# Regrouping the filler steps of a four-layer transformer stack: values' sums off VectorE, a norm moved beside the channel mix, more keys beside norms, keys summed in PSUM banks

## The chip, the core and the metric

The kernel runs on one core of one Trainium2 chip, all in float32. The metric is the device time of one execution in microseconds (us). Five engines work side by side, each through its own queue in order: TensorE (PE, with its weight loads shown as PEld), VectorE (DVE), ScalarE (ACT), GpSimd (POOL) and SyncE (SP, which issues all DMAs here). A float32 matmul shows in the profile as two records.

## What is computed

The tokens `x` are 8 sequences of 112 tokens with 512 channels, and the context is 8 x 375 x 512. Four layers follow one another:

```python
x = layer0(x, ctx)        # one-head cross attention, x + alpha * delta
x = layer1(x, state=ctx)  # RWKV block: time mix, then channel mix
x = layer2(x, state=ctx)  # the same, other weights
x = layer3(x, ctx)        # two cross attentions and an MLP
# an RWKV block
xa = ln(x); sx = shift(xa) - xa
xw, xk, xv, xr, xg = (xa + sx * (maa_f + tanh((xa + sx*maa_x) @ w1) @ w2[f]) for f in "wkvrg")
w = exp(-exp(decay + tanh(xw @ d1) @ d2)); r, k, v = xr @ Wr.T, xk @ Wk.T, xv @ Wv.T; g = silu(xg @ Wg.T)
s = k[:, None] * v[None, :] + w[:, None] * s      # per token, 32 heads of 16 x 16
x = x + group_norm(r @ (u * k v + s)) * g @ Wo.T
xc = ln(x); x = x + sigmoid(xr2 @ fWr.T) * (relu(xk2 @ fWk.T)**2 @ fWv.T)
# layer 3, twice, then the MLP: 16 heads of 128; one extra key and value (bias_k, bias_v)
h = ln(x); x = x + softmax((h @ wq + bq) @ keys.T / sqrt(128)) @ values @ wo + bo
x = x + gelu(ln(x) @ w_fc1 + b1) @ w_fc2 + b2
```

## The kernel before

Channels lie on the 128 partitions, in four blocks; tokens lie along the rows. The 896 tokens are worked on in two halves of 448 (`NH`), each of four sequences.

**Values and keys of layer 3.** They depend on the context alone. So `values()` (L788) is a generator that makes them early, and its steps are drawn one at a time as filler (`fill(n)`, L119) wherever layers 1 and 2 leave TensorE without work. Products of 2 x 2 blocks are made with seven block products in place of eight (the sums of weights and of context blocks that this needs are made beforehand). A unit of seven steps is k1, k6, k7 (one bank that keeps growing, copied by ACT at each step), k2, k8, and k5 and k9 (`last_two`, L895), which run between the first steps of the unit after. Two banks take turns. The sum for k2 is an ACT copy and a POOL addition (L966, L967); those for k5 and k9 are DVE additions that read the bank (L898, L902). Results go to DRAM (`store`). When the weights change, `relay` (L820) replaces them piece by piece: each of its stages (POOL sums L829 to L845, loads L807) is issued in the program right after the step that it names (`after`, L919).

**The scan.** `time_mix` (L538) has 64 steps per layer. Each multiplies a broadcast row of v by k (DVE, L675, `kv`, from a PSUM copy `vp` made by ACT, L576 and L577), runs the recurrence along tokens (DVE, L679, `st`), multiplies by r (POOL, L683, `rs`) and sums on TensorE (L656). About two filler steps are drawn in each. Here the order on each engine is the order of the program; elsewhere a scheduler sets each engine's order at build time from what is ready.

**Turned weights.** Wg and Wv of layers 1 and 2 have their columns put into another order in blocks of 128 x 128: a copy by ACT (L407) and a reordering copy back by POOL (L408), 32 of each per layer.

**Mixing.** `mixes(h, fills)` (L416) makes the norm and the five mixed inputs of one half. For the second half the filler is the first half's own projections, and `fills` says how many steps are drawn at each place.

**Channel mix and layer 3.** `channel_mix` (L708) ends with eight groups of output matmuls fv. Then `layer3` starts, with new tile pools. `attention` (L1084) normalizes x in two halves (`layer_norm_half`, L163) with filler from `first_keys`: the 14 steps of the keys of one pair of batches, made by `seven` (L1004): two banks in turn, two ACT copies and five DVE additions for each half of the rows. Eight batches follow for each of four groups of heads; in each, 4 heads go through scores (L1201), softmax (L206), transposes (L1204) and the product with the values (L1214). The key steps of later pairs run in between.

Of the kernel before, what the change touches and what calls it, by code (L numbers as in the profile page):

```python
# [108 lines left out]
def tile_kernel(ctx: ExitStack, tc: tile.TileContext, d: dict, out: bass.AP):  # L109
# [22 lines left out]
    ident = const.tile([P, P], F32, name="ident")  # L132
    make_identity(nc, ident)
# [18 lines left out]
    def project(ps, w, rhs, evacuate, name, hs=(0, 1)):  # L152

        for h in hs:
            for o in range(NC):
                p = mm(ps, f"ps_{name}_{o}_{h}")[:, :NH]
                for k in range(NC):
                    nc.tensor.matmul(
                        p, w[:, k, o * P : (o + 1) * P], rhs(k, h), start=k == 0, stop=k == NC - 1
                    )  # L160
                evacuate(o, h, p)

    def layer_norm_half(ps, work, y, h, scale, offset, name, room=None, bank=None, fills=(2, 2, 4), small_tag="rstd"):  # L163

        def small(tag, what):
            if room is not None:
# [23 lines left out]
        nc.vector.tensor_mul(y, y, rstd.unsqueeze(1).to_broadcast([P, NC, NH]))  # L192
        for c in range(NC):
            nc.scalar.activation(
                y[:, c, :], y[:, c, :], AF.Identity, bias=column(offset, c), scale=column(scale, c)
# [20 lines left out]
    def layer0():  # L216
# [3 lines left out]
        with (  # L220
# [4 lines left out]
        ):  # L225
            w_q, w_k = weight("L0_xattn_w_q"), weight("L0_xattn_w_k")
# [144 lines left out]
    def time_mix_inputs(n, pre, names, ones_t, first, k, v, r, g, decay, rows):  # L371
# [7 lines left out]
        with (  # L379
# [22 lines left out]
            for f in "gv":  # L402
                for o in range(NC):
                    for c in range(NC):
                        w = ws[f][:, c, o * P : (o + 1) * P]
                        t = work.tile([P, NH], F32, tag="e", name=f"turn{f}{n}_{o}_{c}")[:, :P]
                        nc.scalar.copy(t, w)  # L407
                        nc.gpsimd.tensor_copy(w.rearrange("p (q h r) -> p q h r", q=4, h=HB), turned(t))  # L408
# [49 lines left out]
            def projections(h, xw, xg):  # L458
# [4 lines left out]
                td = one.tile([P, NH], F32, tag="td", name=f"td{n}_{h}")  # L463
# [68 lines left out]
            following = projections(1, *mixes(1, (2, 1, 2, 1, 1, 0, 0, 0)))  # L532
# [175 lines left out]
    def channel_mix(n, pre, names, first):  # L708
        with (
# [49 lines left out]
            project(ps, f_v, lambda c, h: halves(kk[:, c, :], h), add, f"fv{n}")  # L759

    def rwkv_layers():
        with tc.tile_pool(name="rc", bufs=1) as one:
# [5 lines left out]
            with tc.tile_pool(name="rs", bufs=1) as setup:  # L768
# [8 lines left out]
                nc.vector.tensor_sub(less_mean_h, ident, mean_h)  # L777
# [10 lines left out]
    def values():  # L788
# [31 lines left out]
        def relay(at, old, new):  # L820
# [5 lines left out]
            for y, o, k in ((a11, 0, 0), (a21, 1, 0), (a22, 1, 1)):  # L826
                raw(y, at, o, k)
            yield "k1"
# [9 lines left out]
            new.update(k1=a11, k6=old["k6"], k7=old["k1"], k2=old["k7"], k8=old["k8"], k5=old["k9"], k9=old["k2"])  # L838
# [55 lines left out]

        def last_two(u, f, u2, u3, s, at):  # L895
            p = bank(u, f, f"k5_{u}")
            product(p, block(at), s["k5"])
            nc.vector.tensor_add(u3, p, u3)  # L898
# [3 lines left out]
            nc.vector.tensor_add(u2, p, u2)  # L902
# [14 lines left out]
        before, steps, following = iter(()), iter(()), None  # L917

        def after(what):  # L919
            nonlocal following  # L920
            if what == following:
# [9 lines left out]
        for u, (at, unit) in enumerate(units):  # L931
# [13 lines left out]
            elif unit == UNITS - 1 and at != 1:  # L945
                following = ready
            if unit % 3 == 0:
# [16 lines left out]

            y = shaped(pool.tile([P, C], F32, tag="k2", name=f"k2_{u}"), f)
            nc.scalar.copy(y, p)  # L966
            nc.gpsimd.tensor_add(p1, y, p1)  # L967
# [14 lines left out]
    def weight_sums(pool, tag, w, u):  # L982


        if tag == "wv":
            y = pool.tile([P, NC, C], F32, tag=tag, name=f"ws{u}")
# [74 lines left out]

    def quarters(y):
# [21 lines left out]
    def attention(i, h_in, work, kv, ps, ps2, keep, mlp_norm):  # L1084
# [9 lines left out]
        def key_pieces(gr, b, w, kts):  # L1094
# [3 lines left out]
            if ("wk", i, gr, b) in shared:  # L1098
                for j in range(2):
                    kts.append(kv.tile([P, HG, T], F32, tag="kt", name=f"k{u}_{j}", bufs=3))  # L1100
# [4 lines left out]
            cx = kv.tile([P, NC, S], F32, tag="cx", name=f"cx{u}", bufs=2)  # L1105
# [8 lines left out]
            kt = [kv.tile([P, HG, T], F32, tag="kt", name=f"k{u}_{j}", bufs=3) for j in range(2)]  # L1114
            kts += kt

            def put(j, o, p, y):
                dst = kt[j][:, o, :S]
                if y is None:
                    nc.scalar.copy(dst, p)  # L1120
# [298 lines left out]
```

## Time and profile before

| | us |
|---|---|
| median of 3 runs | 3005.23 |
| lowest, highest | 2998.66, 3009.64 |
| the profiled execution, its time | 3006.6 |
| the profiled execution, its span | 3004.8 |
| PE busy in it | 2874.8 |
| DVE busy | 1713.4 |
| ACT busy | 862.4 |
| POOL busy | 732.9 |

The rough order in the span: layer 0 up to 159 us, layer 1's mixing up to 364, its scan to 632, its output and channel mix to 801, the same for layer 2 with its scan from 1003 to 1282 and its end at 1470, the two attentions of layer 3 from there, with the second norm at 2127, and the MLP from about 2810. A row of the instructions in order of time gives start, length, engine, line, operation, output and inputs, the count, and in brackets how long the engine was idle before it and what released it. A row of waits gives the total, the number and the longest. A stage's row gives busy times and, after them, the clock that TensorE was granted as a share of full speed.

### The profile page before, as it was taken

How to read it: one execution, taken by the hardware profiler on the slowest of the kernel's cores; microseconds unless marked ns; L12 is line 12 of the kernel's file. 1: busy time of each engine (PE TensorE's matmuls, PEld its weight loads, DVE VectorE, ACT ScalarE, POOL GpSimd, SP SyncE). 2: the span in 40 equal slices, each digit the busy share in tenths (PEclk: the TensorE clock that was granted, in tenths of full speed). 3: DMA queues.
4: the chain of work that ended last, by engine and by line, in shares of the span. 5: the costliest groups of instructions: out<-in, count | busy, mean ns of one | idle time of the engine just before them, and what ended most of it. 6: DMA issues, size and time to landing. Idle time of an engine off the chain costs nothing.

```text
span 3004.8 us, 29759 instructions
## 1 busy us (share of the span) xinstructions
PE 2874.8 (96%) x10130; PEld 1571.3 (52%) x10130; DVE 1713.4 (57%) x2588; ACT 862.4 (29%) x1750; POOL 732.9 (24%) x636
## 2 busy tenths in 40 slices
PE   8989999998999998999899999999899999999999
PEld 4734443343444433346456666656465666656544
DVE  1464198956343588844366555646755565646455
ACT  2123354423243344422132122212221221212311
POOL 3142057534221366632200101020001001010030
PEclk9989999999999999999999999999999999999999
DMA  7421398843311788744225252434243433432110
GB/s 252 148 88 45 122 291 264 250 129 118 95 62 55 223 240 264 229 137 132 85 87 169 90 165 96 138 105 145 70 128 106 138 117 121 139 102 90 45 57 25
DMA packets 199319, 402.91 MB, mean 134 GB/s; under 512 B 33288, under 2 KB 119592, under 8 KB 192384
## 3 DMA queue, kind: packets, MB, share of 16 engines
q1 hardware_dynamic: 199168, 401.01, 42.9%
q8 instruction: 81, 1.33, 0.2%
q14 instruction: 70, 0.57, 0.1%
HBM read 323.16 MB, written 77.91 MB: 133 GB/s over the span
## 4 chain that ended last, share of the span: by engine, by line
PE 50%; DVE 2%; ACT 1%; issue 1%; POOL 0%; DMA 0%; DVEq 0%; ACTq 0%; POOLq 0%
PE av L1214 6%; PE sc L1201 5%; PE ps_k1k L1017 5%; PE ps_k7k L1017 5%; PE ps_k5k L1017 5%; PE pt L1204 3%; PE ps_k6k L1017 2%; PE ps_k7q L1017 2%; PE ps_k5q L1017 2%; PE ps_k5o L1017 1%; PE ps_k1o L1017 1%; PE ps_k7o L1017 1%; PE ps_k1q L1017 1%; PE ps_k5fc L1017 1%; PE ps_k7fc L1017 1%; PE ps_k6q L1017 1%
## 5 line engine op out<-in xcount | busy, mean ns | idle before, releaser
L873 PE MATMUL ps_vk<-wv,cv 128*128 128x512 f32 x1336 | 613.8, 608 | 49.7 <-DVE k L902 12.2
L873 PEld LDWEIGHTS ps_vk<-wv,cv 128*128 128x128 f32 x1336 | 250.8, 193 | 393.1 <-issue 300.9
L210 ACT ACTIVATE prob<-sc,top 112x376 f32<-112x376 f32 (+1 forms) x264 | 152.1, 576 | 712.2 <-DVE top L207 590.9
L683 POOL TENSOR_TENSOR rs<-st,r 128x896 f32<-128x896 f32 x128 | 246.9, 1929 | 281.1 <-DVE st L679 164.1
L679 DVE TENSOR_TENSOR_SCAN st<-decay,kv 128x904 f32<-128x904 f32 x128 | 260.3, 2034 | 9.1
L1201 PE MATMUL sc<-k,q 128*112 128x376 f32 x512 | 200.7, 485 | 1.0 <-ACT prob L210 0.8
L1214 PEld LDWEIGHTS av<-pts,v 125*128 125x128 f32 (+1 forms) x1536 | 184.8, 193 | 29.9 <-DVE pts L1210 15.1
L1214 PE MATMUL av<-pts,v 125*128 125x112 f32 (+1 forms) x1536 | 188.2, 277 | 0.9 <-DMA v<-wvs 0.9
L1194 POOL COPY k<-over_k 128x4 f32<-128x4 f32 x64 | 15.9, 253 | 679.3 <-PE sc L1201 611.0
L1017 PE MATMUL ps_k1k<-cx,w_L_xattn_wk 128*128 128x375 f32 x480 | 177.8, 483 | 1.6 <-ACT rstdk L1035 1.5
L207 DVE TENSOR_REDUCE top<-sc 112x1 f32<-112x376 f32 (+1 forms) x264 | 143.6, 545 | 30.5 <-PE sc L1201 15.9
L956 ACT COPY k<-ps_vk 128x512 f32<-128x512 f32 (+1 forms) x153 | 89.2, 583 | 226.6 <-PE ps_vk L873 204.7
L675 DVE TENSOR_TENSOR kv<-vp,k 128x904 f32<-128x904 f32 x128 | 140.9, 1101 | 17.2 <-ACT vp L577 10.7
L1204 PEld LDWEIGHTS pt<-ident,prob 112*125 112x125 f32 (+1 forms) x768 | 98.2, 176 | 59.5 <-DVE prob L212 32.9
L212 DVE TENSOR_SCALAR prob<-prob,total 112x376 f32<-112x376 f32 (+1 forms) x264 | 118.9, 453 | 7.1
L1017 PEld LDWEIGHTS ps_k1k<-cx,w_L_xattn_wk 128*128 128x128 f32 x480 | 89.7, 192 | 59.7 <-issue 3.3
L1204 PE MATMUL pt<-ident,prob 112*125 112x112 f32 (+1 forms) x768 | 116.1, 272 | 1.9 <-DVE prob L212 1.9
L577 ACT COPY vp<-vj 128x896 f32<-128x896 f32 x124 | 112.8, 910 | 16.3 <-DMA vj<-rows 12.4
L967 POOL TENSOR_TENSOR k<-k,k 128x512 f32<-128x512 f32 (+1 forms) x51 | 65.9, 1292 | 200.3 <-ACT k L966 91.4
L1221 DVE TENSOR_TENSOR ctxt<-av,bv 128x448 f32<-128x448 f32 x64 | 40.0, 625 | 127.6 <-PE av L1214 127.6
L1201 PEld LDWEIGHTS sc<-k,q 128*112 128x112 f32 x512 | 78.8, 176 | 41.4 <-ACT prob L210 6.4
L1017 PE MATMUL ps_k7k<-cs,wsk 128*128 128x375 f32 x240 | 88.5, 480 | 0.6 <-DVE k L1122 0.6
(375 smaller groups left out, 4713.8 us busy)
## 6 DMA issues: line engine op xcount, KB each, us to landing
vj<-rows SPq DMA_DIRECT2D x124, 448.0 KB
cv<-blocks SPq DMA_DIRECT2D x181, 251.5 KB
cs<-blocks SPq DMA_DIRECT2D x120, 375.0 KB
wvs<-k SPq DMA_DIRECT2D x128, 256.0 KB
v<-wvs SPq DMA_DIRECT2D x64, 512.0 KB
cx<-in_ctxT SPq DMA_DIRECT2D x38, 750.0 KB
v<-wvs SPq DMA_DIRECT2D x64, 252.0 KB
wvs<-k SPq DMA_DIRECT2D x64, 224.0 KB
```

Source lines behind the costliest of these rows:

```text
L207: nc.vector.tensor_reduce(top, scores, AX.X, ALU.max, negate=True)
L210: nc.scalar.activation(prob, scores, AF.Exp, bias=top, accum_out=total)
L212: nc.vector.tensor_scalar(prob, prob, total, None, ALU.mult)
L577: nc.scalar.copy(vp[:, :, 1:], by_batch(vjs.pop((c, j))))
L675: nc.vector.tensor_mul(flat(kv), flat(vp), flat(k[:, c]))
L679: nc.vector.tensor_tensor_scan(flat(st), flat(decay[:, c]), flat(kv), 0.0, ALU.mult, ALU.add)
L683: nc.gpsimd.tensor_mul(by_batch(rs), st[:, :, :L], by_batch(r[:, c, :]))
L873: nc.tensor.matmul(to, left, right, start=start and n == 0, stop=k == 1, skip_group_check=True)
L1017: nc.tensor.matmul(to, lhsT, rhs, start=start and k == 0, stop=k == 1, skip_group_check=not start)
L1201: nc.tensor.matmul(sc, q[:, o, tok], kt[:, o, :], start=True, stop=True)
L1204: nc.tensor.transpose(pt[t][:nt, o, :], prob[:, t0 : t0 + nt], ident[:L, :L])
L1214: nc.tensor.matmul(av[:, o, :], v[:nt, t, o * HD : (o + 1) * HD], pts[:nt, t, o, :], start=t == 0, stop=t == 2,)
```

## The change

- **Values:** k5 and k9 are now added as k2 is: an ACT copy into a buffer (two of them) and a POOL addition. A stage of `relay` is issued only when two further steps have followed the one that it names.
- **Turned weights:** halves of 128 x 1024 are copied by ACT and put back in the new order by DVE: 4 of each per layer. The buffer is another, `half`.
- **Mixing of the second half:** one more projection step is drawn, after the second block of channels. `td` takes the place of `t4` in memory.
- **Channel mix of layer 2:** the eight output groups are split by halves of tokens. The four of the second half are filler for the first half of layer 3's first norm, up to its division; the tiles for this are two weight buffers. Scale and offset follow at the start of layer 3 (`scale_by_channel`).
- **Layer 3:** `first_keys` makes two pairs of batches (28 steps) and the norms draw up to 20 (first attention) or 32 of them. Key tiles have four buffers, not three. Keys are made by the new `chained`: for each half of the rows one bank keeps growing and another takes the rest; at `busy` times ACT copies and POOL adds, at others DVE adds. Some tiles move to a pool `near`, which comes first in memory, where `values` had its tiles. The identity matrix is made three times, where it is used, and the sums of weights for keys and fc1 share other buffers.

```diff
             for f in "gv":
-                for o in range(NC):
-                    for c in range(NC):
-                        w = ws[f][:, c, o * P : (o + 1) * P]
-                        t = work.tile([P, NH], F32, tag="e", name=f"turn{f}{n}_{o}_{c}")[:, :P]
-                        nc.scalar.copy(t, w)
-                        nc.gpsimd.tensor_copy(w.rearrange("p (q h r) -> p q h r", q=4, h=HB), turned(t))
+                for half in range(2):
+                    w = ws[f][:, 2 * half : 2 * half + 2].rearrange("p c n -> p (c n)")
+                    t = work.tile([P, NC, NH], F32, tag="half", name=f"turn{f}{n}_{half}")
+                    t = t.rearrange("p c n -> p (c n)")[:, : 2 * C]
+                    nc.scalar.copy(t, w)
+                    nc.vector.tensor_copy(
+                        w.rearrange("p (a q h r) -> p a q h r", q=4, h=HB, r=4),
+                        t.rearrange("p (a h q r) -> p a q h r", q=4, h=HB, r=4),
+                    )
...
-                td = one.tile([P, NH], F32, tag="td", name=f"td{n}_{h}")
+                td = one.tile([P, NH], F32, tag="t4", name=f"td{n}_{h}")
...
-            following = projections(1, *mixes(1, (2, 1, 2, 1, 1, 0, 0, 0)))
+            following = projections(1, *mixes(1, (2, 1, 2, 1, 1, 1, 0, 0)))
...
-            project(ps, f_v, lambda c, h: halves(kk[:, c, :], h), add, f"fv{n}")
+            def values_pieces(h):
+                for o in range(NC):
+                    project(ps, f_v, lambda c, h: halves(kk[:, c, :], h), add, f"fv{n}", [h], [o])
+                    yield
...
+                for _ in values_pieces(0):
+                    pass
+                filler = values_pieces(1)
+                fill(1)
...
+                layer_norm_half(ps, work, y, 0, None, None, "ln3_1", ([sq], None), None, (1, 1, 1))
+                for _ in filler:
+                    pass
+                shared["normed"] = y
...
+        def add(y, p, u, f, what):
+
+            z = shaped(pool.tile([P, C], F32, tag="k2", name=f"{what}_{u}", bufs=2), f)
+            nc.scalar.copy(z, p)
+            nc.gpsimd.tensor_add(y, z, y)
+
         def last_two(u, f, u2, u3, s, at):
             p = bank(u, f, f"k5_{u}")
             product(p, block(at), s["k5"])
-            nc.vector.tensor_add(u3, p, u3)
+            add(u3, p, u, f, "k5")
...
-            nc.vector.tensor_add(u2, p, u2)
+            add(u2, p, u, f, "k9")
...
-            if what == following:
+            made.append(what)
+            while following in made[:-2]:
+                del made[: made.index(following) + 1]
                 following = next(steps, None)
...
+    def chained(ps, work, w, s, b, t, n, dst, u, busy):
...
+            for p, left, right, start, to, add in (
+                (grows, lambda k: w[:, k], b11, True, p1, None),
+                (other, lambda k: s()[0][:, k], t[0], True, dst(1, 2 + m), None),
+                (grows, lambda k: s()[1][:, k], t[1], False, u2, None),
+                (other, lambda k: s()[3][:, k], b22, False, dst(1, m), u2),
+                (grows, lambda k: s()[2][:, k], t[2], False, u3, None),
+                (other, lambda k: w[:, 2 + k], b21, True, dst(0, m), p1),
+                (grows, lambda k: w[:, 2 + k, 256:], t[3], False, dst(0, 2 + m), None),
+            ):
...
+                if add is None or busy:
+                    nc.scalar.copy(to, p)
+                    if add is not None:
+                        nc.gpsimd.tensor_add(to, to, add)
+                else:
+                    nc.vector.tensor_add(to, p, add)
+                if to is u3:
+                    (nc.gpsimd if busy else nc.vector).tensor_add(dst(1, 2 + m), dst(1, 2 + m), u3)
...
         def first_keys():
+
             w_ks.append(key_weight(0))
-            yield from key_pieces(0, 0, w_ks[0], kts)
+            for b in (0, 2):
+                yield from key_pieces(0, b, w_ks[0], kts)
+                made.append(b)
...
-        fill(3)
-        layer_norm(ps, work, h_in, scaled[:, :NC], scaled[:, NC : 2 * NC], f"ln3_{i}", ([halves(room, h) for h in range(2)], t_h), ln_bank)
+        for h in range(2):
+            if i == 1 and not h:
+                scale_by_channel(halves(h_in, 0), shared.pop("normed"), *scales)
+            else:
+                fill(2)
+                layer_norm_half(ps, work, halves(h_in, h), h, *scales, f"ln3_{i}", room, ln_bank, (3, 3, 4))
+        fill(8)
         token_sums(nc.vector, *quarters(h_in), t_h)
```

## The prediction

> **What bounds the kernel now.** I read the busy shares first, then the busy time by stage, then who waits for whom, and last the instructions in order of time around each long wait. TensorE is busy for 96% of the span, so only time in which it does nothing useful can be won.
>
> ```profile
> PE 2874.8 (96%) x10130; PEld 1571.3 (52%) x10130; DVE 1713.4 (57%) x2588; ACT 862.4 (29%) x1750; POOL 732.9 (24%) x636
> ```
>
> The stages below are, in order: the two scans (64 steps each), the first and the second norm of layer 3, two stretches inside the channel mixes, and the last mixing of layer 1. The columns are length, busy time of PE, PEld, DVE, ACT and POOL with instructions, granted clock, DMA share and GB/s.
>
> ```profile
> 364.00:632.00 268.00, 254.76 (x764) 102.60 (x762) 239.09 (x178) 130.43 (x241) 167.89 (x99) 0.99 0.89 262
> 1003.00:1282.00 279.00, 258.20 (x765) 102.82 (x763) 239.19 (x178) 131.01 (x241) 167.75 (x99) 0.99 0.85 249
> 1470.00:1535.00 65.00, 49.52 (x128) 25.13 (x128) 42.52 (x50) 18.29 (x29) 12.60 (x11) 0.89 0.33 102
> 2127.00:2182.00 55.00, 47.13 (x125) 23.96 (x124) 37.65 (x47) 17.99 (x26) 5.60 (x7) 0.94 0.22 67
> 710.00:735.00 25.00, 16.64 (x33) 7.05 (x33) 18.68 (x20) 7.75 (x23) 24.46 (x28) 0.80 0.41 119
> 1380.00:1395.00 15.00, 10.01 (x67) 9.34 (x67) 7.99 (x14) 2.06 (x4) 1.24 (x1) 0.77 0.31 103
> 276.00:291.00 15.00, 14.04 (x30) 6.60 (x30) 14.22 (x21) 0.00 (x0) 10.39 (x9) 0.66 0.00 0
> ```
>
> Both scans hold the same work, yet one takes 268 and the other 279 us, with DVE at 239 us in each. Everywhere else in this table DVE or POOL is full while the clock is below one. The attention between the norms shows PE at 50 of 50 us in every slice: nothing is to be won there.
>
> ```profile
> PE ps_vk L873 <- DVE k L902: 12.2, 7, 2.7
> PE ps_vk L873 <- DVE k L898: 10.3, 8, 5.3
> PE mean_ln L178 <- POOL k L1194: 9.2, 1, 9.2
> PE ps_k6q L1017 <- DVE t_h L1000: 8.7, 2, 5.1
> ```
>
> L902 and L898 are the two DVE additions of the values' steps k9 and k5. The next rows are PE in order of time, with the wait in brackets; the two ACT and POOL rows explain the first.
>
> ```profile
> 724.20 3.78 PE L873 MATMUL ps_vk<-wv,cv 128*128 128x512 f32 x4 [7.03 <-ACT k L973]
> 727.77 2.80 PE L158 MATMUL ps_fk<-xk,w_L_xattn_fWk_None 128*128 128x448 f32 x4
> 730.41 1.88 PE L873 MATMUL ps_vk<-wv,cv 128*128 128x512 f32 x4
> ...
> 718.60 0.30 ACT L407 COPY turng<-w_L_xattn_Wg_None 128x128 f32<-128x128 f32 x1 [5.56 <-POOL w_L_xattn_Wg_None L408]
> ...
> 1384.99 9.22 PE L873 MATMUL ps_vk<-cv,wv 128*128 128x125 f32 x64 [5.27 <-DVE k L898]
> ...
> 1479.42 1.83 PE L178 MATMUL mean_ln<-t_h,mean_c 128*128 128x448 f32 x2 [9.25 <-POOL k L1194]
> ...
> 2164.57 3.33 PE L1017 MATMUL ps_k6q<-t_h,ws1q 128*128 128x448 f32 x4 [5.12 <-DVE t_h L1000]
> ```
>
> A long wait also slows what follows: 3.78 us for work that takes 1.88 us six us later. From undisturbed stretches I take what a matmul record costs PE: 0.43 us at 512 columns (16 in 7.13), 0.376 at 448 (64 in 24.22), 0.316 at 375 (4 in 1.27), 0.10 for the scan's packed sums (16 in 1.71).
>
> **Scans: k5 and k9 leave DVE.** PE's own work in one scan is 494 x 0.43 + 246 x 0.10 + 24 x 0.376 = 246 us, so 22 and 33 us, 55 together, are lost. DVE spends 64 x 2.03 + 64 x 1.10 on scan and product, 18 on reciprocals and 35 x 0.68 = 24 on these additions, which stand in its queue between a product and a 2 us scan. They become an ACT copy (the k2 row, 0.58 us) and a POOL addition (1.27 us): DVE 239 to 215, ACT 130 to 151, POOL 168 to 212. All are below PE's 246, so PE should set the pace. Behind the new ACT copy stands the copy of the next v row, which waits for DVE's product anyway; the copy buffer holds two, so ACT waits for POOL only if POOL is two additions late. What stays lost: the waits for group norms and for the last sums (about 7 us), bursts around an exchange of weights, and something new there. The exchange is now two steps late: three additions, one copy and three 512 KB loads per exchange, the loads in SP's queue beside the rows of the scan. The load issued at 1136.69 was needed at 1145.68, after a wait of 2.60 us; two steps are 4 us, so 0 to 4 us more at each of two exchanges, while POOL's own exchange sums no longer stand in front of the scan's products. I take 22 of the 55 us, 4 us of new weight waits being inside; bounds -38 and +10.
>
> Here a rule speaks against the change. The row: an addition of 128x512 takes 0.68 us on DVE (L898) and 1.27 on POOL (L967). The Trainium skill, "GPSIMD Engine Reference", section 4.1, says elementwise work belongs on VectorE, GpSimd being about twice as slow with two inputs. The ratio agrees, 1.9. By the rule 102 moved additions cost 102 x 0.59 = 60 us; by the trace they cost PE nothing while POOL has 100 us idle in a scan, and the sum is -22. I go by the queue that is full.
>
> **Turned weights.** 32 ACT copies and 32 POOL copies of 0.30 us a layer become 4 and 4, POOL's going to DVE. At 712 to 729 the small pairs wait for each other, and POOL has shifts of 9 us in front, so the evacuation of k8 (L973) stood behind a copy that waited 5.56 us for POOL: 7.03 us, and 1.9 + 1.1 us of half speed after it. With two whole halves and two buffers nothing in ACT's queue waits for another engine for Wg. New on DVE are two reorderings of 128x1024 beside the 10.5 us of xk: no such row, between 0.6 us (half of a pass at kv's 1.10 us for 904) and 1.7 us each (eight times the 0.21 us reordering of 128x128); I take 1.1, on the path if they come before xk. Sum -9, bounds -11 and -2. Wv's halves come at 758 under PE's full stretch: nothing, and if not covered 2 us. In layer 1 they fall at 47 to 65 us under attention 0: nothing.
>
> **Other norms.** At 1384.99 the k5 addition stood behind xk's eight operations on DVE. ACT is idle then (1380 to 1390), so 5.27 goes, with 2.1 of slow clock (64 records at 0.111 are 7.1, not 9.22): -7. At 825.40 the k9 addition did the same for 2.18; next late is the operand xx itself: -2. The extra filler in the second mixing puts the r projection (12 us) between mixings 1 and 2; at 276 to 291 DVE is full and PE has about 7 us of work, but the projection then no longer stands under DVE's tail. Each layer -4 to +4, I take -1: -2. The shared buffer of td and t4 has both readers apart by six pieces; nothing, at most 1 us. Three identities instead of one: POOL rows of 0.20 and 0.29 us at the very start, under loads; nothing.
>
> **First norm of layer 3.** From 1470 to k6q's end of waiting at 1518 PE has 48 us and does 17.7 of keys, 3.0 of sums, 6.0 of queries and 1.3 of scores: 28. So 20 are lost, and k6q runs 1.3 us slow. After: half 0's chain (sums 1.9, mean 0.8, less 2.0, square 1.7, sums 1.9, variance 0.8, root 0.6, reciprocal 2.95, product 2.0, about 15) lies beside the last four output steps (12 us), and half 1's 15 us plus scale 2.7 and token sums 4.3 beside up to 28 key steps of 1.26. The loads of the first keys (at 1472 before) go to memory that the values used, so they land under the channel mix; the norm's two tiles take weight buffers, so wk is loaded once fr is done (1446), 24 us ahead of its use. POOL gets the keys' twelve additions of 375 (about 0.93 us each, from 1.27 at 512), which only the attention waits for. Left: 1 to 2 us for the last addition to x, and copies behind ACT's square (1.7) or scale (2.7): 6. Sum -15, bounds -20 and -4. **Second norm:** 37.4 us with 28.2 of work, and 3.4 slow after it; left 4.6: -8, bounds -11 and 0.
>
> **Keys growing in banks.** Matmuls stay 28 a pair. In the attention DVE gives up 10 additions of 0.55 for 6, ACT goes from 4 copies of 0.47 to 10; PE is full there, gain none. A bank is free when its copy ends: 0.47 us inside the other bank's 1.26. If ACT is late by one exponential (0.58 + 0.20), that still fits. But two batches of each attention now stand without keys to fill them. The last such batches (2793 to 2806) show waits of 0.80, 0.70, 1.16 and 0.90: about 2 us a batch, less in the first attention, where 8 steps are left: +4.
>
> **The sum:** -22 -9 -7 -2 -2 -15 -8 +4 = -61. The profiled execution took 3006.6 us; it stands 1.4 above the median, so 3005.2 - 61, rounded to 2945.
>
> On the clock, the Trainium skill, "TensorE: Matmul & The Clock Gate", "What's actually happening", has half speed until about 3.4 us of work: at most 1.7 us a gap. At 724 the trace has 3.0 us lost, and at 282 to 290 a clock of 0.52 with no gap in PE's rows. By the rule the terms above would be 2 us smaller; I keep the trace.
>
> **Rivals.** Half the gain: the order of instructions is worked out anew at build time, the ACT copies fall behind norms' operations, and the weight loads cost 4 us each. Half of each term gives -30 + 6, about 2980; for it speaks that ACT already made PE wait (L973, 9.5 us), against it that ACT has over 100 us free per scan. No change: the key steps stand beside the norms already (14 of them do), and the uncovered batches give it back; scans stay on the load of rows. About 3000. Slower: POOL becomes the scans' bound through its order. Every moved addition waits for PE's step and ACT's copy, and the scan's products stand behind it. With a wait W each, POOL needs 212 + 35 W; with the other terms at -39 the change loses once 2 x (212 + 35 W) exceeds 547 + 39, at W = 2.3 us. At 2.7 us it is 3032. For it: POOL is full at exchanges already; against: the 18 present additions of a scan have 2.7 us of idle before them in all.
>
> **Numbers.** Forecast 2945, own range 2920 to 2970: 0.62. Half gain 0.20, of it 0.17 faster by over 0.5%. No change 0.09, slower 0.09. What a measurement can tell is 0.5%, 15 us: faster below 2990. Faster 0.79, same 0.12, slower 0.09. The range that leaves out 2 in 10 runs from 2915 to 2993.
>
> **What would show it.** Scans near 262 us each with no DVE addition among PE's waits; POOL near 212 in each. No ACT copy waiting on POOL near 716. PE busy from the channel mix into the keys, and k6q within 3 us of its forerunner. Wrong if the scans keep 268 and 279, if PE waits for ACT key copies by over 10 us in the norms, or if the attention falls below 49 of 50.

## The result, and the profile after

The changed kernel takes 2975.27 us (median of 4 runs, 2970.53 to 2976.49) against 3007.43 us for the kernel before (4 runs): a ratio of 0.9893, 95% interval 0.9866 to 0.9920. That is 32 us faster, half of the forecast 61. The time lies 5 us outside the prediction's own range (2920 to 2970) and inside its wider one (2915 to 2993); the rival "half the gain" had named 2980, which is nearer than 2945. The profiled execution has a span of 2972.9 us against 3004.8, and its differences are the ones split up below.

The page's first line and the stretches that answer to those shown before, in this order: scan 1, scan 2, the first norm of layer 3, the second norm, the channel mix of layer 1. Columns as before.

```profile
PE 2865.5 (96%) x10130; PEld 1561.6 (53%) x10130; DVE 1608.9 (54%) x2350; ACT 999.1 (34%) x1992; POOL 876.6 (29%) x702
```
```profile
363.00:626.00 263.00, 253.00 (x764) 103.17 (x762) 221.27 (x144) 150.18 (x277) 210.60 (x134) 0.99 0.91 265
983.00:1253.00 270.00, 255.14 (x765) 103.48 (x763) 221.51 (x144) 149.81 (x277) 209.01 (x133) 0.99 0.88 256
1439.00:1485.00 46.00, 38.80 (x102) 20.60 (x101) 22.49 (x16) 17.76 (x32) 26.26 (x24) 0.85 0.55 184
2095.00:2136.00 41.00, 38.49 (x119) 21.64 (x117) 26.30 (x20) 23.13 (x41) 15.30 (x15) 1.00 0.39 125
700.00:725.00 25.00, 21.33 (x52) 9.27 (x51) 21.64 (x13) 9.83 (x16) 21.96 (x16) 1.00 0.50 158
```

Over the whole span 105 us of DVE work have become 137 us of ACT and 144 us of POOL work. The scans take 263 and 270 us for the same matmuls that took 268 and 279: POOL is at 210, as forecast, but only the first is near the forecast 262. The second norm is nearly full, the channel mix has its clock back, and the first norm has 7 us of idle PE and a clock of 0.85.

What PE waits for now (us in total, times, longest):

```profile
PE ps_vk L905 <- DMA wv<-in_L_xattn_wv: 12.7, 4, 7.9
...
PE ps_vk L905 <- ACT k L998: 5.5, 4, 1.7
...
PE ps_vk L905 <- POOL wv L866: 4.8, 2, 2.7
...
PE mean_ln L182 <- DVE t_h L180: 4.1, 1, 4.1
```

The 22.5 us behind the two DVE additions and the 9.2 us behind a POOL addition are gone. New are 4.8 us for POOL's sums of the next weights. The waits for ACT are more in number (24 for 20), but 4 us less in all (27.9 for 31.9).

**Where the time went, by stage.** Both kernels issue the same 10,130 matmuls. I gave each matmul the PE time of the prediction's undisturbed records (0.43 us at 512 columns, 0.376 at 448, and so on), cut both traces where the same amount of this work was done, and took length minus work as the time lost in a stage. The table has those losses in us; the columns are the kernel before, the changed one, and six of the experiments (e1 to e12 are explained below).

| stage | before | changed | e1 | e4 | e5 | e7 | e10 | e11 |
|---|---|---|---|---|---|---|---|---|
| layer 0 and first half of layer 1's mixing | 48.1 | 46.7 | 44.3 | 45.2 | 44.2 | 44.4 | 46.5 | 45.6 |
| rest of layer 1's mixing | 24.1 | 24.3 | 22.9 | 24.0 | 24.0 | 23.0 | 24.2 | 24.1 |
| scan 1 | 23.6 | 18.7 | 26.5 | 19.7 | 18.4 | 18.3 | 20.2 | 21.0 |
| channel mix 1 | 16.2 | 9.1 | 14.9 | 9.1 | 9.1 | 20.9 | 9.1 | 9.1 |
| mixing of layer 2 | 26.3 | 19.4 | 24.2 | 22.2 | 19.4 | 19.8 | 19.7 | 20.7 |
| scan 2 | 34.6 | 25.5 | 35.5 | 24.0 | 24.4 | 23.0 | 24.0 | 21.0 |
| channel mix 2 | 11.9 | 9.0 | 12.2 | 9.0 | 9.0 | 9.0 | 9.0 | 9.0 |
| first norm of layer 3 | 23.4 | 16.2 | 16.5 | 22.2 | 12.0 | 14.5 | 2.8 | 2.8 |
| first attention | 23.0 | 26.6 | 25.8 | 23.1 | 28.3 | 27.6 | 29.1 | 26.7 |
| second norm and batches after it | 23.2 | 21.0 | 20.4 | 18.9 | 21.0 | 20.5 | 17.9 | 13.9 |
| second attention | 17.6 | 19.4 | 19.5 | 17.9 | 19.9 | 18.9 | 19.1 | 17.4 |
| last batches and their norm | 14.4 | 18.2 | 19.5 | 14.0 | 17.6 | 13.6 | 15.0 | 14.5 |
| MLP | 4.4 | 4.7 | 5.5 | 4.4 | 5.5 | 7.0 | 4.4 | 5.0 |

A stage with unchanged code still moves: scan 2 of the seven kernels with the changed kernel's scan spans 23.0 to 25.5, the last batches 13.6 to 18.2 in six of them. Channel mix 2, at 9.0 in most of them, is at 13.8 in e9 and 12.4 in e12, which the table leaves out. So I read no stage difference under 2 us, and none in the last batches.

### The profile page after: what moved, and what is told of

Its sections match the earlier page's. It is cut to its first block, busy times and chain, and to the rows that moved or that the text cites. A ratio compares the mean times of both kernels' runs of the same rounds, so it can differ in the third digit from the quotient of the medians.

```text
span 2972.9 us, 29802 instructions
## 1 busy us (share of the span) xinstructions
PE 2865.5 (96%) x10130; PEld 1561.6 (53%) x10130; DVE 1608.9 (54%) x2350; ACT 999.1 (34%) x1992; POOL 876.6 (29%) x702
## 3 DMA queue, kind: packets, MB, share of 16 engines
q1 hardware_dynamic: 199168, 401.01, 43.1%
## 4 chain that ended last, share of the span: by engine, by line
PE 80%; DVE 8%; POOL 4%; DMA 3%; ACT 3%; issue 2%; SPq 0%; DVEq 0%; POOLq 0%; ACTq 0%
PE ps_vk L905 13%; PE ps_k1k L1133 10%; PE ps_k5k L1133 7%; PE av L1302 6%; PE sc L1289 5%; PE ps_o L161 3%; PE pt L1292 3%; PE ps_k1q L1060 2%; PE ps_r L484 2%; PE ps_k L484 2%; PE ps_k5q L1060 2%; PE ps_fr L161 2%; PE ps_k7q L1060 2%; PE ps_fk L161 2%; PE ps_k7fc L1060 1%
## 5 line engine op out<-in xcount | busy, mean ns | idle before, releaser
L905 PE MATMUL ps_vk<-wv,cv 128*128 128x512 f32 x1336 | 602.9, 602 | 31.4 <-DMA wv<-in_L_xattn_wv 12.7
L931 POOL TENSOR_TENSOR k<-k,k 128x512 f32<-128x512 f32 (+1 forms) x153 | 202.1, 1321 | 308.1 <-ACT k L930 261.3
L691 DVE TENSOR_TENSOR_SCAN st<-decay,kv 128x904 f32<-128x904 f32 x128 | 260.7, 2037 | 16.5 <-POOL rs L695 3.8
L1282 POOL COPY k<-over_k 128x4 f32<-128x4 f32 x64 | 13.8, 224 | 604.7 <-PE sc L1289 576.7
L1133 PE MATMUL ps_k1k<-cs,wsk 128*128 128x375 f32 x480 | 179.8, 483 | 1.5 <-ACT p1k L1136 1.5
L930 ACT COPY k<-ps_vk 128x512 f32<-128x512 f32 (+1 forms) x153 | 89.2, 583 | 183.1 <-PE ps_vk L905 180.1
L998 ACT COPY k<-ps_vk 128x512 f32<-128x512 f32 (+1 forms) x153 | 89.1, 582 | 157.6 <-PE ps_vk L905 151.7
L1292 PEld LDWEIGHTS pt<-ident_l,prob 112*125 112x125 f32 (+1 forms) x768 | 97.9, 176 | 73.0 <-DVE prob L220 43.9
L1292 PE MATMUL pt<-ident_l,prob 112*125 112x112 f32 (+1 forms) x768 | 121.2, 277 | 3.3 <-DVE prob L220 2.1
L1133 PEld LDWEIGHTS ps_k1k<-cs,wsk 128*128 128x128 f32 x480 | 90.0, 191 | 60.1 <-issue 2.4
L1140 DVE TENSOR_TENSOR k<-ps_k5k,u2k 128x375 f32<-128x375 f32 x52 | 28.5, 549 | 159.2 <-PE ps_k5k L1133 158.2
```

The costliest lines, as they stand in the source:

```text
L691: nc.vector.tensor_tensor_scan(flat(st), flat(decay[:, c]), flat(kv), 0.0, ALU.mult, ALU.add)
L905: nc.tensor.matmul(to, left, right, start=start and n == 0, stop=k == 1, skip_group_check=True)
L931: nc.gpsimd.tensor_add(y, z, y)
L1133: nc.tensor.matmul(y, lhsT, rhs, start=start and k == 0, stop=k == 1, skip_group_check=True)
L1292: nc.tensor.transpose(pt[t][:nt, o, :], prob[:, t0 : t0 + nt], ident[:L, :L])
```

## The experiments

The times, each with its ratio to runs of the kernel before on the same chip:

| run | what differs | us | ratio, 95% interval |
|---|---|---|---|
| e1 | changed, additions of k5 and k9 on DVE | 2997.04 | 0.9966 (0.9952 to 0.9980) |
| e2 | changed, exchange issued promptly | 2970.97 | 0.9878 (0.9861 to 0.9894) |
| e3 | changed, first keys' additions on DVE | 2967.91 | 0.9867 (0.9851 to 0.9884) |
| e4 | changed, all keys as before | 2970.95 | 0.9877 (0.9861 to 0.9893) |
| e5 | changed, first norm after the channel mix | 2970.54 | 0.9877 (0.9862 to 0.9891) |
| e6 | changed, one pair of first keys | 2980.11 | 0.9909 (0.9894 to 0.9923) |
| e7 | changed, turned weights in small pieces | 2977.57 | 0.9911 (0.9886 to 0.9936) |
| e8 | changed, last output step earlier | 2974.42 | 0.9890 (0.9875 to 0.9905) |
| e9 | e2, e3 and e5 together | 2966.55 | 0.9851 (0.9834 to 0.9868) |
| e10 | e9, first keys' operands in early memory | 2959.42 | 0.9834 (0.9821 to 0.9847) |
| e11 | e10, grown keys beside norms only | 2952.07 | 0.9809 (0.9793 to 0.9825) |
| e12 | e11, half 0's norm beside the channel mix | 2964.36 | 0.9860 (0.9841 to 0.9880) |

The changed kernel has 0.9893 (0.9866 to 0.9920). Only e1, e10 and e11 have intervals clear of that one. What the others show is read from their stages and rows, each from a single trace.

**e1, the values' additions on DVE.**

```diff
-            add(u3, p, u, f, "k5")
+            nc.vector.tensor_add(u3, p, u3)
-            add(u2, p, u, f, "k9")
+            nc.vector.tensor_add(u2, p, u2)
```

> The changed kernel with the values' steps k5 and k9 added on DVE again, everything else kept. Theory A (the moved additions gave the two scans what they gained, 4.8 and 9.1 us, and the late exchange costs on top of it): the scans' lost time goes from 18.7 and 25.5 back to about 24 and 35 us or more, some 2989 us in all. Rival B (the scans gained because the exchange of weights is issued two steps later, and moving the additions brought nothing): scans stay within 3 us of 18.7 and 25.5, 2972 to 2978 us.

Theory A holds: 22 us of the 32 are gone by the medians, so the moved additions are about two thirds of the gain. By stages the scans lose 7.8 and 10.0 us more, the channel mixes 5.8 and 3.2, layer 2's mixing 4.8. These sum to 31.6, but the traced execution (3003.64 us) is the slowest of e1's eight, 6.6 us above their median. So the stages tell where the gain lies, not its size: nearly half of it is outside the scans. PE in channel mix 1 of e1, and one scan:

```profile
724.99 3.78 PE L905 MATMUL ps_vk<-wv,cv 128*128 128x512 f32 x4 [5.84 <-DVE k L936]
```
```profile
360.00:630.00 270.00, 255.02 (x762) 101.76 (x760) 239.00 (x178) 130.80 (x241) 167.74 (x99) 0.99 0.88 258
```

At the place where PE waited 7.03 us for an ACT copy before, it now waits 5.84 us for the k5 addition, which stands on DVE behind twelve operations of xk and xr. The turned weights were regrouped in this run too; alone that gained 1.3 us here.

**e7, the turned weights in small pieces** (the 16 ACT and 16 POOL copies of each weight, as before the change).

> The changed kernel with the turned weights again in 16 pieces each, copied by ACT and reordered by POOL. Theory A (these small pairs were the 7.03 us wait at 724): the channel mix of layer 1 loses 14 to 17 us and not 9, with an ACT copy of the values waiting for POOL, about 2982 us. Rival B (the wait was that of a DVE addition as much, as the run with DVE additions shows with 5.84 us at the same place; with those gone nothing is left to wait): 9 to 11 us lost there, 2974 to 2977 us.

Channel mix 1 loses 20.9 us, more than theory A allowed. First ACT's row, then PE's (line numbers are three lower here):

```profile
711.27 0.30 ACT L416 COPY turng<-w_L_xattn_Wg_None 128x128 f32<-128x128 f32 x1 [7.96 <-POOL w_L_xattn_Wg_None L417]
```
```profile
714.64 3.52 PE L902 MATMUL ps_vk<-wv,cv 128*128 128x512 f32 x4 [4.22 <-ACT k L1009]
...
721.84 3.78 PE L902 MATMUL ps_vk<-wv,cv 128*128 128x512 f32 x4 [2.93 <-ACT k L927]
```

The two parts need each other: with the small pieces ACT's queue waits for POOL, with the additions on DVE PE waits for DVE. Either part undone brings back 6 to 12 us of this stage. The total rose by 2 us only; other stages, of unchanged code, were better by up to 4.6 us each, so for this run the stage is the reading.

**e2, the exchange of weights without its delay.**

```diff
-            while following in made[:-2]:
+            while following in made:
```

> The changed kernel with each step of an exchange of weights issued as soon as its step is done, not two steps later. Theory A (the delay is what the exchange waits for: 2.68 us for POOL in scan 1, 2.16 for POOL and 4.52 for DMA in scan 2, and 3.4 us of half speed in each): these waits fall to at most 3 us in all, the scans gain 6 to 9 us together, 2966 to 2969 us. Rival B (the delay pays for itself, because POOL's sums of 2.4 us no longer stand in front of the scan's products and of the moved additions): PE waits for ACT copies or POOL products instead and the time is 2975 us or more.

Neither. The waits for POOL's weight sums went, as A says, but ACT's copies and group norms took their place in scan 1 (lost 20.6 against 18.7; scan 2, 21.1 against 25.5). Over all kernels with the moved additions the two scans together lose 41.3 to 44.2 us with the delay (seven kernels, mean 43.1) and 41.7 to 44.2 without it (five, mean 42.8). The delay is worth nothing either way, and the 4.3 us of the medians cannot be put on it.

**e4, all keys as before** (each product in a bank of its own, `seven` in place of `chained`; two pairs of first keys stay).

> The changed kernel with the keys of layer 3 made as before (each product in a bank of its own) and everything else of the change kept. Theory A (keys growing in banks hold PE for ACT's copy where ACT is late, 1.55 us and 6.8 us of half speed at 2734 in the last batches, and 1.30 us in each norm): the last batches lose 4 us less, the attention 2 us less, about 2969 us. Rival B (they free DVE where DVE is the norm's bound): the two norms lose 5 us more and the total is 2975 to 2985 us.

Both, in different stages. The first norm loses 6 us more, as B says; the attentions 3.5 and 1.5 us less, as A says. The edit also takes the first keys' additions off POOL; e3, next, does that alone and loses nothing more in the first norm, so the 6 us are the banks'. Growing in banks pays beside the first norm and costs in the attentions. That the cost comes from ACT, busy there with exponentials, is the likely reason and not shown.

**e3, the first keys' additions on DVE** (`busy` false everywhere).

> The changed kernel with the first keys' additions on DVE out of PSUM, not an ACT copy and a POOL addition. Theory A (POOL at work slows DVE's sums over SBUF from 0.62 to 1.6 us, and that is why the norms gained only half of what was forecast): beside keys the sums take 0.62 us, the first and second norm lose 4 to 6 us less together, about 2970 us. Rival B (DVE's queue is the norms' bound, and six more additions of 0.55 us a pair stand in it): the norms lose 4 to 6 us more, about 2980 us.

7 us by the medians. By stages 3.6 are in the second norm and behind it and nothing in the first, so A can hold for one of the two norms only. DVE's first sum of squares in the first norm, in the kernel before and in the changed one, then two rows of POOL, beside that sum and beside DVE's product in the second norm:

```profile
1485.07 0.63 DVE L174 TENSOR_TENSOR t_h<-room 128x448 f32<-128x448 f32 x1 [1.76 <-ACT room L185]
```
```profile
1454.36 1.57 DVE L178 TENSOR_TENSOR t_h<-room 128x448 f32<-128x448 f32 x1 [3.88 <-ACT room L189]
```
```profile
1454.19 1.25 POOL L1036 TENSOR_TENSOR ws2q<-w_L_xattn_wq 128x512 f32<-128x512 f32 x1
...
2112.26 2.38 POOL L1142 TENSOR_TENSOR k<-k,u3k 128x375 f32<-128x375 f32 x1 [0.34 <-ACT u3k L1136]
```

The same sum takes 0.63 us alone and 1.57 when POOL is at work; POOL's addition of 375, at most 1.0 in the kernel before, takes 2.38 beside that product. In the first norm POOL's sums of weights do this, and those stay in e3; in the second norm it is the keys' additions, and there e3 has all six sums at 0.61 to 0.63. How much of the 3.6 us this is stays open, since e3 takes the first keys' additions off ACT as well as off POOL. PE's two waits at the end of this norm in the changed kernel are one of each kind, and neither is over 0.2 us in e3:

```profile
2133.16 1.53 PE L1133 MATMUL ps_k5k<-cx,w_L_xattn_wk 128*128 128x375 f32 x4 [1.30 <-ACT k L1136]
...
2137.59 4.78 PE L1060 MATMUL ps_k1q<-h_in,w_L_xattn_wq 128*128 128x448 f32 x12 [1.47 <-DVE bv L1242]
```

**e5, the first norm behind the channel mix.**

```diff
-            if n == 1:
+            if n:
                 project(ps, f_v, lambda c, h: halves(kk[:, c, :], h), add, f"fv{n}")
```

(Half 0 is then normed behind the channel mix in the same way as half 1.)

> The changed kernel with the first norm of layer 3 made whole after the channel mix, nothing of it beside the last output steps; two pairs of keys stay its filler. Theory A (half 0 beside the output steps hides most of its 15 us): the stretch from the end of the channel mix to the first scores loses 23 to 26 us, not 16, and the time is 2980 to 2985 us. Rival B (half 0's work only moves the wait: its reciprocal of 2.95 us stands on DVE in front of the last output product, PE waits 4.12 us and runs 13.7 us at half speed): the stretch changes by 2 us at most, 2973 to 2977 us.

Both fall: the norm loses 12.0 us and not 16.2, though the attention behind it loses 1.7 more, which leaves 2.5 us. Putting half 0 beside the output steps gained nothing and was rather a loss; e12 below shows it again. **e8** asks whether it is the order on DVE:

```diff
-                layer_norm_half(ps, work, y, 0, None, None, "ln3_1", ([sq], None), None, (1, 1, 1))
+                layer_norm_half(ps, work, y, 0, None, None, "ln3_1", ([sq], None), None, (1, 2, 0))
```

> The changed kernel with one number changed: the last output step of the channel mix is issued ahead of the sum for the variance, so that its product on DVE stands in front of the reciprocal of half 0. Theory A (that reciprocal is what makes the mean of half 1 wait 4.12 us): the wait falls below 2 us, half speed at 1445 from 13.7 to at most 6.8 us, 2969 to 2972 us. Rival B (the key steps could not start sooner anyway, since POOL's sums of the key weights begin at 1445.9): PE waits for those sums instead, 2974 to 2976 us.

B in its time, though the wait is for a load. In the changed kernel DVE's reciprocal does hold the last product, and POOL's addition after it, and with it PE (DVE, POOL, PE). That addition took 1.13 or 1.14 us the seven times before; beside DVE's next product it takes 2.84, and ends 0.99 us after that product:

```profile
1439.45 2.95 DVE L195 RECIPROCAL rstd__ln<-rstd__ln 128x448 f32<-128x448 f32 x1
1442.31 0.56 DVE L769 TENSOR_TENSOR rr<-ps_fv,rr 128x448 f32<-128x448 f32 x1
1442.79 2.01 DVE L196 TENSOR_TENSOR y_ln<-y_ln,rstd__ln 128x1792 f32<-128x1792 f32 x1
```
```profile
1442.95 2.84 POOL L770 TENSOR_TENSOR x<-x,rr 128x448 f32<-128x448 f32 x1 [4.08 <-DVE rr L769]
```
```profile
1446.60 1.83 PE L182 MATMUL mean_ln<-t_h,mean_c 128*128 128x448 f32 x2 [4.12 <-DVE t_h L180]
```

With that order mended, PE in e8 waits 1.21 us for the mean, but then 4.23 for the second key step's operand, and half speed lasts 17.1 us and not 13.7:

```profile
1441.51 0.99 PE L182 MATMUL mean_ln<-t_h,mean_c 128*128 128x448 f32 x2 [1.21 <-DVE t_h L180]
1446.73 2.84 PE L1133 MATMUL ps_k5k<-cs,wsk 128*128 128x375 f32 x4 [4.23 <-DMA cs<-blocks]
```

SP's rows of the changed kernel tell why: wq waits 22.6 us for the sum of half 0's squares, which lie in a weight buffer, and cs, behind it in the queue, is issued only when the channel mix's last addition to x is done (a wait of 4.2 us).

```profile
1414.21 0.33 SPq L127 DMA_DIRECT2D w_L_xattn_wk<-in_L_xattn_wk  x1
1437.21 0.33 SPq L127 DMA_DIRECT2D w_L_xattn_wq<-in_L_xattn_wq  x1
...
1445.82 1.98 SPq L1193 DMA_DIRECT2D cs<-blocks  x4
```

**e6, one pair of first keys.**

> The changed kernel with one pair of first keys beside each norm, the second pair made inside its batch as before. Theory A (the second pair covers the norms): 14 steps of 1.26 us run out before the token sums, PE waits 5 us in each norm and loses 2 us of clock after it, 2985 to 2990 us. Rival B (what the second pair covers, the batches without keys give back): norms 10 us worse in all, batches 6 to 9 us better, 2975 to 2979 us.

The second norm and the batches behind it lose 7.3 us more (28.3 against 21.0), the first norm nothing. So the second pair pays at the second norm, while at the first PE waits for the start of the keys and not for their end. The attentions do not give the 6 to 9 us back that B had (27.2 and 20.2 against 26.6 and 19.4).

**e9, three parts taken back together.**

> The changed kernel with three parts taken back together: exchange issued promptly, first keys' additions on DVE, first norm of layer 3 whole after the channel mix. Theory A (each acts in its own stage and they add up): by the stages of the single runs 2.6 us in the scans, 3.6 in the second norm and the queries behind it, 4.2 in the first norm, 10 in all, 2965 us; by the medians of the single runs 16 us, 2959 us. Rival B (what the single runs gained was mostly where the half speed happened to fall): 2968 to 2971 us.

2966.6: between A by stages and B; single medians do not add up. The first norm, at 8.6, still has one long wait, 5.29 us for cs. **e10** moves memory alone:

```diff
-            t = [shared["pool"].tile([P, 3, 2, CT], F32, tag="cs", name=f"cs{u}_{j}", bufs=4) for j in range(4)]
+            t = [near.tile([P, 3, 2, CT], F32, tag="cs", name=f"cs{u}_{j}", bufs=4) for j in range(4)]
-            h_in = near.tile([P, NC, N], F32, name="h_in")
+            h_in = keep.tile([P, NC, N], F32, name="h_in")
```

(cy and the sums of wk go to `near` as well, q and room to `keep`.)

> The kernel of e9_three, with the memory of layer 3 laid out the other way round: the first keys' operands (cs, cy) and the sums of their weight lie in the part that is free early, and the norm's own tiles (h_in, room, q) in the part that the channel mix still uses. Theory A (what is left of the first norm is the start of the keys: PE waited 4.71 us for cs, loaded only after the channel mix's last addition, and POOL's sums of wk came behind it): the keys start right behind the channel mix, its stretch loses 5 to 8 us, not 12, about 5 us less than e9_three. Rival B (keys that start sooner are used up sooner, and PE waits for the token sums instead): within 2 us of e9_three.

Theory A, and more: the norm loses 2.8 us. The 7 us between the medians of e9 and e10 agree; in the traces channel mix 2 differs too, by 4.8. cs is loaded at 1372.82, under the channel mix, and POOL sums wk before the additions to x. The 46 us from 2 us before the first key step on, which had 38.80 of PE in the changed kernel, now have 44.95, at full clock:

```profile
1372.82 2.30 SPq L1193 DMA_DIRECT2D cs<-blocks  x4
```
```profile
1436.00:1482.00 46.00, 44.95 (x136) 24.98 (x135) 29.85 (x32) 20.67 (x34) 9.51 (x12) 1.00 0.49 155
```

**e11, grown keys beside the norms only** (`seven` when `gr or b >= BH`).

> The kernel of e10_near_operands, with only the first keys, those beside the norms, growing in banks; all keys made inside a batch are made as before the change. Theory A (in a batch the grown keys cost PE waits behind ACT, which has 10 copies a pair and not 4): the first attention loses 23 us and not 26.6, the second 18 and not 19, some 4 to 5 us less than e10_near_operands. Rival B (the batches without keys cost it, and the run with all keys made as before only moved it): within 1.5 us of e10_near_operands.

Theory A: 7 us by the medians, and 8.1 by the stages from the first attention to the second (2.4, 4.0 and 1.7). The last of these is small, but the second attention loses 17.4 to 17.9 us in every kernel without grown keys in its batches (before, e4, e11, e12) and 18.9 to 20.2 in every other. The first attention stays at 26.7, above the 23.0 before the change. The batches that now have no keys beside them do not explain it: e4 has them too and loses 23.1, and e12, with the same attention as e11, is within 1 us of the kernel before. What does explain it stays open. e11 is the fastest kernel here: 2952 us, 1.9% below the kernel before.

**e12, half 0's norm beside the channel mix again, on e11.**

> The kernel of e11_mixed_keys with half 0 of the first norm of layer 3 put back beside the last output steps, as the change has it. Theory A (half 0 there cost 4 us only because its two tiles held weight buffers and the key operands lay in late memory; with the operands early it is harmless): the first norm loses 2 to 4 us as without it, 2950 to 2954 us. Rival B (it costs by itself, through the reciprocal of 2.95 us and the sums that stand on DVE in front of the last additions to x, and POOL and DVE slow each other on them): PE waits for the mean of half 1 by 2 us or more and the norm loses 6 to 9 us, 2955 to 2958 us.

12 us slower by the medians, 15 by the ratios; the norm loses 15.1 us, more than B said. The rows are of ACT, POOL and PE:

```profile
1451.45 0.47 ACT L1136 COPY k<-ps_k5k 128x375 f32<-128x375 f32 x1 [8.30 <-POOL x L770]
1451.81 2.71 ACT L202 ACTIVATE h_in<-y_ln,scaled 128x448 f32<-128x448 f32 x4
```
```profile
1448.51 2.90 POOL L770 TENSOR_TENSOR x<-x,rr 128x448 f32<-128x448 f32 x1
```
```profile
1451.97 2.09 PE L1133 MATMUL ps_k5k<-cy,wsk 128*128 128x375 f32 x4 [3.96 <-ACT k L1136]
```

B's delay is there: behind the reciprocal, and beside DVE's product, POOL's last addition to x ends 5.9 us after the last output matmul, and in e11 2.0 us. But PE does not wait for the mean. ACT's copy into the key tile k waits for that addition, and the scaling of half 0 and the next copies stand behind it; PE waits 3.96 and then 2.54 us for them. That k's memory, which e10 did not move, is freed by the addition would explain the copy's wait; the trace shows only the wait. So A falls for this layout. What half 0 beside the channel mix would do with the key tiles early too was not tried and stays open.

## Why the prediction was half right

The direction and the main cause were right; of the forecast 61 us, 32 came. The terms in turn:

- **Scans, -22 forecast, -14.0 measured** (4.9 and 9.1). The cause was right: in e1's trace the scans lose 17.8 us more, and POOL is at 210 with DVE at 221. The step that failed is "what stays lost", the waits for group norms and last sums of about 7 us. Those are 6.4 us, but PE's waits fell only from 13.8 to 10.8 us in the first scan and from 21.5 to 15.6 in the second. Of the 14.7 us behind DVE none is left. The waits behind ACT, 14.9 us before, are still 14.2, and the forecast counted only the group norms' share of them (3.8); POOL (7.5 us, before 2.2) and loads (4.7, before 3.5) have the rest. The slower rival did not come: POOL is idle for 53 us of scan 1 in all, 1.5 us for each of 35 moved additions if it were all such waits, and not 2.3. The order in ACT's queue makes these waits: a copy of a product stands behind the copy of a v row, which waits for DVE's product (ACT, then PE; first the kernel before, then the changed one):

```profile
1196.17 0.91 ACT L577 COPY vp<-vj 128x896 f32<-128x896 f32 x1
1197.01 0.58 ACT L966 COPY k<-ps_vk 128x512 f32<-128x512 f32 x1
...
1197.64 7.11 PE L873 MATMUL ps_vk<-wv,cv 128*128 128x512 f32 x12 [2.34 <-ACT k L966]
```
```profile
1171.86 0.91 ACT L589 COPY vp<-vj 128x896 f32<-128x896 f32 x1
1172.71 0.58 ACT L930 COPY k<-ps_vk 128x512 f32<-128x512 f32 x1
...
1173.34 5.42 PE L905 MATMUL ps_vk<-wv,cv 128*128 128x512 f32 x12 [1.76 <-ACT k L930]
```

- **The rule against POOL additions** (half as fast as DVE) had asked for 60 us of cost. The runs decide against it: 22 us gained, since the queue that was relieved held PE up. The scan's DVE operations were not slowed by POOL, 2.04 and 1.11 us with it and without.
- **Turned weights, -9 forecast, -7.1 measured**, right in size and half right in cause: e1 and e7 show that it takes both parts. I booked the 7 us on the copies alone, and overlooked that DVE's queue would hold the same product. The two reorderings of a weight took 0.68 us each on DVE, not 1.1.
- **Other norms**: channel mix 2 gave 2.9, not 7: the wait of 5.27 us is gone, but 2.37 us for xk is new. Layer 2's mixing gave 6.9, not 3; in e1's trace 4.8 of it are the additions', where I had counted a single wait of 2.18. That the two sum to 9.8 with 10 forecast is luck.
- **First norm, -15 forecast, -7.2 measured.** The failed step is "the loads of the first keys go to memory that the values used, so they land under the channel mix". Of the operands it was true of cx alone; cs was issued at 1445.82. The second is "half 0's chain lies beside the last four output steps": it lay there, but its reciprocal and its weight buffers delayed what came next, and e5 is 4.2 us better without it, 2.5 with the attention behind. With early operands e10 loses 2.8, which is better than the 8 us that the forecast left.
- **Second norm, -8, and batches without keys, +4.** The norm did as forecast or better: PE is busy for 38.49 of 41 us. Call lead the time by which the changed kernel comes sooner to the same amount of PE work: from the end of the first attention to behind the norm it grows from 33.1 to 43.7 us, and over the next batches it falls back to 37.8. The term mis-sized is the price behind the norms: 3.6 us in the first attention, 5.9 here, 1.8 in the second. It was booked on the batches without keys, but e4 has these and loses in the attentions what the kernel before loses. The step that failed is "PE is full there, gain none": e11 puts 8.1 us from the first attention to the second on the keys growing in banks.
- **POOL additions beside a norm** were booked as "only the attention waits for" them. e3 shows that DVE's sums pay for them in the second norm.
- **A reading.** "Everywhere else in this table DVE or POOL is full" holds for two of the five rows (24.46 of 25 us of POOL, 14.22 of 15 of DVE). At 1380 DVE had 7.99 of 15 us, in the norms 42.52 of 65 and 37.65 of 55: there the busy share does not explain PE's waits.

Of the tells, scans near 262 came for one scan only; POOL near 212, no ACT copy waiting on POOL near 716, k6q without a wait behind k1q (1488.69), and no DVE addition among the waits all came. PE from the channel mix into the keys was not full, and that was the place to look.

## What to carry to other kernels

Work taken from a queue that holds PE up to two idle ones paid here at twice the duration, but the wait it removes can be shared: look for what else stands in front of the same buffer, and count the waits for the next queue that are there already. Filler beside a norm helps only if its operands are there: follow each of its loads back to the memory it lands in and the last reader of that memory, and give early memory to what is needed first. Ask of every instruction moved to POOL which two-input DVE operations run at that moment.

## What the runs showed of the hardware

DVE and POOL slow each other on some operations only. In the changed kernel sums of two SBUF operands (128x448) take 0.62 us alone and 1.0 in the median beside an addition of POOL, mostly at most 1.7 and 2.65 at worst; the scaling of probabilities takes 0.42 and 0.97 (medians). Operations with an operand in PSUM (1.11 us, 0.62 us), the scan (2.04) and the reciprocal (2.95) keep their time. The Trainium skill, "SBUF — State Buffer", "Who interferes with whom", says of such sums that a DVE instruction with two SBUF inputs contends with a GpSimd instruction that reads SBUF. The same page's "Summary: rules for kernel authors" says that the second one to issue is blocked until the first has finished. The rows above agree: DVE's sum that starts at 1454.36, under POOL's sum that ends at 1455.44, ends 0.49 us after it, and POOL's addition that starts at 1442.95, under DVE's product that ends at 1444.80, ends 0.99 us after it. The scaling has one SBUF input, so the first of these sentences does not cover it. The prediction weighed POOL's speed but not this rule, which bore on the norms.

The clock records of the trace have half speed for 112.6 us of the span before, 81.9 after and 51.2 in e11. The prediction's rows have 3.78 us in such a stretch for what took 1.88 later, so the 31 us less of it are at most some 15 of the 32 us gained. A wait can cost about as much again in speed: at 1445 13.7 us at half speed, so up to 6.8 us lost, come with waits of 1.2 and 4.1 us. The 1.7 us a gap that the prediction set against the trace was an estimate of its own, half of the skill's 3.4 us.
